# A ternary feed-forward kernel: gelu in PSUM in the last block, its last chunk in halves, one more block of x kept on chip, the first result in two pieces

## The chip, the core and the metric

The kernel runs on one core of one Trainium2 chip. The metric is the time of one execution on the device, in microseconds; the figure of a kernel is the median of several executions. The profile is of one further execution, and its span (first to last instruction) is a little shorter than that execution's time. Engines: TensorE (PE, matmuls), VectorE (DVE), ScalarE (ACT), GpSimd (POOL) and SyncE (SP); DMA engines move data between the device memory and the on-chip memory SBUF. PSUM is the on-chip memory that matmuls write.

## What is computed

x has 128 items of 64 channels by 512 features. Each item picks one of 200 condition matrices (64 x 64) by its index and is multiplied by it. The result goes through two ternary linear layers (512 to 2048 to 512) with an exact gelu between them; the output is rounded to 4 bits with one scale for the whole tensor and added to x:

```python
w = weights[conditions]
c = jnp.einsum('bct,bcd->bdt', x, w)
h = ternary_linear(c, W1, b1)            # W -> alpha * sign(W) * (|W| > delta)
h = jax.nn.gelu(h, approximate=False)
y = ternary_linear(h, W2, b2)
scale = jnp.max(jnp.abs(y)) / QMAX + EPS
q = jnp.clip(jnp.round(y / scale), -QMAX, QMAX) * scale
out = x + q
```

The scale is a maximum over all of y, so no output can be written before the last y is known. x is needed twice: at the start of a block, and again at the end for the sum.

## The kernel before

**Tiling.** The 128 items are 16 blocks (NB) of 4 pairs (PAIRS), so a block is 512 tokens (BLK), and its x is 128 partitions x 4 x 512 fp32, 1 MiB. The 2048 hidden units are 16 chunks (NH) of 128. Every fp32 operand of a matmul is split in two parts, high (a rounded copy made by ACT) and low (the remainder, made by DVE), so that each product takes two matmuls.

**A step.** Blocks 0, 1, 13, 14 and 15 run in plain steps, eight(s), one for each block n and chunk hc. A step widens the fp8 weights of the next chunks (widen1, widen2, on POOL), runs layer1 (8 matmuls of 128x512 into a PSUM tile ph), then bend: ACT applies gelu to ph and writes the result to an SBUF buffer hf, ACT copies that to the high part, DVE subtracts for the low part. At the end of the step layer2 runs 8 matmuls for the chunk of two steps ago (LAG = 2) into the four PSUM tiles py of the block. Blocks 2 to 12 (SEVEN) use a scheme with seven products in place of eight; the change doesn't touch them.

**After a block's last chunk** result moves each py to an SBUF tile y with alpha and bias (four DVE operations), and largest takes the maxima. For block 14 this happens in step 1 of block 15. The y of all 15 earlier blocks stay on chip in the pool big; block 15's y stays in PSUM.

**Loads of x for the end.** In block 15, room comes free and x is loaded again: block 0 into a big tile (hc == 0), blocks 1 and 2 into tiles of the pool half (hc == 1, 2), blocks 3 and 4 in quarters into the dead fp8 weights (lend, lines 817 to 821). After the last step blocks 5 and 6 go into the two big tiles of block 15's conditioned input, blocks 7, 8 and 9 into half tiles (split_x, line 999), and blocks 10 to 15 into tiles that come free as results leave. All these DMAs are issued by SP, in the order written, so a load that waits for room holds those behind it.

**The end.** The last three chunks of layer 2 are done pair by pair (lines 977 to 984), the maxima are spread over the partitions by a transpose (spread) and give scale and its inverse; then for each half block ACT computes q = y * inverse into int8, DVE computes q * scale + x into y, and POOL issues the DMA to the output. POOL has at most eight output DMAs on their way.

**Pools.** half has 10 tiles of 128 x 1024 fp32. In block 15 they hold the widened weights of layer 1 and layer 2, hf (two buffers in one tile, line 669), the parts of h, and x. PSUM has eight banks of 128 x 512 fp32: two for ps_c (conditioning), two for ps_h (ph), four for ps_y (py).

**Order.** Instructions of an engine stay in the order in which the program writes them (InOrder); an engine that waits holds everything behind it. All operations are issued through one helper, which is why the profile shows line 55 for nearly everything; tiles are told apart by name.

Of the kernel before, what the change touches and what calls it, by code (L numbers as in the profile page):

```python
# [29 lines left out]
F32 = mybir.dt.float32  # L30
# [5 lines left out]
AF = mybir.ActivationFunctionType  # L36
ALU = mybir.AluOpType
# [3 lines left out]
P = 128  # L41
# [17 lines left out]
def tile_cond_ternary_ffn(  # L59
# [12 lines left out]
    pe, act, dve, pool, sp = (  # L72
        InOrder(tc, e) for e in (nc.tensor, nc.scalar, nc.vector, nc.gpsimd, nc.sync)
    )
    B, C, T = x.shape
    S, _, D = weights.shape
    NT = T // P
    NH = W1.shape[1]
    assert 2 * C == P and 2 * D == P and C == D and W1.shape == (P, NH, NT, P)
    PAIRS = 4  # L80
    BLK = PAIRS * P
    NB = B // (2 * PAIRS)
# [5 lines left out]
    HALF = BLK // 2  # L88
# [5 lines left out]
    ps_c = ctx.enter_context(tc.tile_pool(name="ps_c", bufs=2, space=PSUM))  # L94
    ps_h = ctx.enter_context(tc.tile_pool(name="ps_h", bufs=2, space=PSUM))
# [3 lines left out]
    out_blk = out.rearrange("(n j p) c t -> n (p c) j t", j=PAIRS, p=2)  # L99

    def pair_of_pairs(h):
        return slice(h * PAIRS // 2, (h + 1) * PAIRS // 2)

    def load_x(n):

        xt = big.tile([P, PAIRS, T], F32, tag="big", name=f"xt_{n}")
        for h in range(2):
            js = pair_of_pairs(h)
            sp.dma_start(out=xt[:, js, :], in_=x_blk[n][:, js, :])
        return [xt[:, pair_of_pairs(h), :] for h in range(2)]  # L110

    def half_x(n, h):

        xt = half.tile([P, PAIRS // 2, T], F32, tag="half", name=f"xt_{n}_{h}")
        sp.dma_start(out=xt, in_=x_blk[n][:, pair_of_pairs(h), :])
        return xt

    def split_x(n):

        return [half_x(n, h) for h in range(2)]  # L120
# [14 lines left out]
    for g in range(NG):  # L135
        w = big.tile([P, GH, T], F32, tag="big", name=f"nat1_{g}")
# [6 lines left out]
    for g in range(NG):  # L143
        w = big.tile([P, GH, T], F32, tag="big", name=f"nat2_{g}")
# [36 lines left out]
    diag = const.tile([P, PAIRS, P], F32)  # L181
# [44 lines left out]
        split(pc, *(t[:, :, j * P : (j + 1) * P] for t in two))  # L226


    def spread(top1, out, wide_top):

        dve.tensor_copy(wide_top, top1.to_broadcast([P, P]))
        tops = ps_c.tile([P, P], F32, tag="pc", name=f"tops_{out.name}")
        pe.transpose(tops, wide_top, ident_f)
        return tops

# [21 lines left out]
    def flat(w):  # L257
        return w.rearrange("p a b -> p (a b)")
# [107 lines left out]
    cond = {0: two_next}  # L366


    hidden = {}
    wide1 = {}  # L370
# [30 lines left out]
            pool.tensor_copy(w, w2t[:, hc])  # L401
        wide2[n, hc] = w

    def layer1(n, hc, ph, pieces=1, between=None):

        w = wide1.pop((n, hc))
        for i in range(pieces):
            part = slice(i * BLK // pieces, (i + 1) * BLK // pieces)
            for c in range(NT):
                if between is not None and c == NT - 1:  # L410
                    between()
                for k in range(2):
                    pe.matmul(
                        out=ph[:, part],
                        lhsT=w[:, c, :],
                        rhs=cond[n][k][:, c, part],
                        start=(c == 0 and k == 0),
                        stop=(c == NT - 1 and k == 1),
                    )

    def bend(n, hc, ph, two, hf, engine=dve):
        act.activation(hf, ph, AF.Gelu, bias=b1t[:, hc : hc + 1], scale=alpha[1])
        if engine is None:
            act.copy(two[0], hf)
            open_low[n, hc] = lambda: dve.tensor_tensor(two[1], hf, two[0], ALU.subtract)
        else:
            split(hf, *two, engine)
        hidden[n, hc] = two
# [42 lines left out]
    def early(hc, between=None):  # L471

        slot = (hc + 1) % 5
        if slot < 2:
            ph = ps_h.tile([P, BLK], F32, tag="ph", name=f"ph_0_{hc}")
        else:
            ph = ps_y.tile([P, BLK], F32, tag=f"py{slot - 2}", name=f"ph_0_{hc}")
        layer1(0, hc, ph, 2 if hc == 0 else 1, between)
        waiting[hc] = ph

    def early_bend(hc):
# [187 lines left out]
    hf = ring[:2]  # L669
# [142 lines left out]

    steps = [(n, hc) for n in range(NB) for hc in range(NH)]
    again = []
    dying = [flat(t).bitcast(F32).rearrange("p (j t) -> p j t", j=PAIRS) for t in (w1t, w2t)]

    def lend(t, n, hc):
# [5 lines left out]
    def eight(s):  # L823

        n, hc = steps[s]
        if s + 1 < len(steps):
            ahead = steps[s + 1]
            if ahead[0] not in SEVEN:
                widen1(*ahead)
                lend(0, *ahead)  # L830
            else:
                for g in (2, 3, 0):
                    widen7(0, g)
        widen2(*steps[s + 1 - LAG])
        lend(1, *steps[s + 1 - LAG])
        if n + 1 < NB:
            if hc == 0:
                if n + 1 == SEVEN[0]:
                    extra["x"] = half.tile([P, 2, T], F32, tag="half", name="x_quarters")
                    for j in range(2):  # L840
                        quarter_x(n + 1, j)
                else:
                    x_next.append(load_x(n + 1) if n + 1 < NB - 1 else split_x(n + 1))
                two_next.append(parts7(n + 1) if n + 1 in SEVEN else parts(n + 1))
            if 2 <= hc < 2 + PAIRS:
                fetched.append(fetch(n + 1, hc - 2))
            if 7 <= hc < 7 + PAIRS:
                place(hc - 7, fetched[hc - 7 - PAIRS])
        if n == NB - 1 and hc == 0:
            again.append(load_x(0))  # L850
        if n == NB - 1 and hc in (1, 2):
            again.append(split_x(hc))
        ph = ps_h.tile([P, BLK], F32, tag="ph", name=f"ph_{n}_{hc}")
        layer1(n, hc, ph)
        two = half.tile([P, 2, BLK], F32R, tag="half", name=f"h_{n}_{hc}")
        bend(n, hc, ph, [two[:, k, :] for k in range(2)], hf[hc % 2])
        if s + 1 < len(steps) and steps[s + 1][0] in SEVEN and n not in SEVEN:
            widen7(0, 1)
        if n + 1 < NB and 8 <= hc < 8 + PAIRS:
            j = hc - 8  # L860
            if n + 1 in SEVEN:
                condition7(n + 1, j, extra["x"][:, j % 2, :], two_next[-1])()
                if j + 2 < PAIRS:
                    quarter_x(n + 1, j + 2)
            else:
                condition(n + 1, j, pair_of(x_next[-1], j), two_next[-1])
            cond[n + 1] = two_next[-1]
        if hc == LAG:
            for j in range(PAIRS):
                largest(n - 1, j)  # L870
        if n + 1 == SEVEN[0]:
            if hc == 2:
                extra["making"] = combine()
            if hc in (3, 4, 5, 6):
                next(extra["making"])
        if s == len(steps) - 1:
            return
        if s == NH + 1:
            alpha_2()
        layer2(*steps[s - LAG])  # L880
        if steps[s - LAG][1] == NH - 1:
            for j in range(PAIRS):
                result(n - 1, j)
# [64 lines left out]
    s = NH  # L948
    finish = None
    parting = []  # L950
    while s < len(steps):
        n, hc = steps[s]
# [14 lines left out]
    n = NB - 1  # L967
# [9 lines left out]
    for j in range(PAIRS):  # L977
        for hc in range(NH - 1 - LAG, NH):
            layer2(n, hc, [j])
        y = ypsum[n][j]  # L980
# [6 lines left out]
    ymax1 = const.tile([P, 1], F32)  # L987
# [1 line left out]
        ymax1, ymax.rearrange("p n j -> p (n j)")[:, n * PAIRS : NB * PAIRS + 1], AX.X, ALU.max  # L989
    )  # L990
    scale = const.tile([P, 1], F32, name="scale")
    tops = spread(ymax1, scale, diag[:, 0, :])
    dve.tensor_reduce(scale, tops, AX.X, ALU.max)
    dve.tensor_scalar(scale, scale, 1.0 / QMAX, EPS, ALU.mult, ALU.add)
    inverse = const.tile([P, 1], F32)
    dve.reciprocal(inverse, scale)


    xs = again + [split_x(len(again) + i) for i in range(3)]
    quant = flat(diag).bitcast(I8).rearrange("p (k t) -> p k t", k=PAIRS)  # L1000
    AHEAD = len(xs)
    for n in range(NB):

        while len(xs) < min(AHEAD + 3 * n // 2, NB):
            xs.append(load_x(len(xs)))
        for h in range(2):


            q = quant[:, h * PAIRS // 2 : (h + 1) * PAIRS // 2, :]
            if n < NB - 1:  # L1010
                y = res = ys[n][:, pair_of_pairs(h), :]
                act.activation(flat(q), flat(y), AF.Identity, scale=inverse)
                dve.scalar_tensor_tensor(
                    flat(y), flat(q), scale, flat(xs[n][h]), ALU.mult, ALU.add
                )
            else:
                res = xs[n][h]
                for k in range(PAIRS // 2):
                    y = ypsum[n][h * PAIRS // 2 + k]
                    act.activation(q[:, k, :], y, AF.Identity, scale=inverse)  # L1020
                    dve.scalar_tensor_tensor(
                        res[:, k, :], q[:, k, :], scale, res[:, k, :], ALU.mult, ALU.add
                    )
            pool.dma_start(out=out_blk[n][:, pair_of_pairs(h), :], in_=res)
# [44 lines left out]
```

## Time and profile before

| | |
|---|---|
| median of 3 runs | 1062.01 us (1061.17 to 1062.29) |
| profiled execution, its time | 1061.88 us |
| its span | 1059.5 us |
| mean granted TensorE clock | 0.969 |
| busy: PE | 986.9 us (93%) |
| busy: PEld (weight load) | 864.2 us (82%) |
| busy: DVE, ACT, POOL | 609.5, 611.3, 627.2 us |
| bytes moved | 62.19 MB, of which 44.34 MB read and 16.78 MB written in device memory |
| DMA of x (xt<-in_x, 512 KB each) | 36 issues, median 6.9 us to landing |
| DMA of results (out<-y, 512 KB each) | 30 issues, median 12.5 us to landing |

Busy time is the sum of an engine's instructions over the span. The page also cuts the span into 40 equal slices, each of 26.5 us, and gives each engine's busy share there in tenths; a row PEclk gives the granted clock, a row DMA the mean busy share of the 16 DMA engines. In a list of groups or a timeline, "out<-in" names the tile written and the tiles read, "128x512" is partitions by elements, and the bracket at the end is how long the engine sat idle before the instruction and who released it. The operations that the change touches, by kind and size, with their mean length:

| engine, operation | size | count | mean ns |
|---|---|---|---|
| ACT gelu, ring<-ph | 128x512 | 80 | 779 |
| ACT cast, h<-ring (SBUF to SBUF) | 128x512 | 256 | 621 |
| ACT cast, x<-pc (PSUM to SBUF) | 128x512 | 20 | 583 |
| ACT copy, ring<-z (PSUM to SBUF) | 128x512 | 88 | 588 |
| ACT copy, ring<-xy (PSUM to SBUF) | 128x256 | 176 | 370 |
| DVE subtract, h<-ring,h | 128x512 | 252 | 771 |
| DVE subtract, x<-pc,x | 128x512 | 20 | 684 |
| DVE subtract, xb<-pc,xb | 128x256 | 44 | 413 |
| ACT q, diag<-y | 128x1024 | 30 | 1148 |
| ACT q, diag<-py | 128x512 | 4 | 684 |
| DVE sum, y<-diag,scale,xt | 128x1024 | 26 | 1282 |
| DVE sum, xt<-diag,scale,xt | 128x512 | 4 | 748 |

### The profile page before, as it was taken

The page shows a single profiled execution, that of the slowest core. Times are in us where ns is not written, and L with a number is a line of the kernel's source. Part 1 is how long each engine was busy: PE and PEld are TensorE (multiplying, and loading weights), DVE is VectorE, ACT ScalarE, POOL GpSimd, SP SyncE. Part 2 cuts the span into 40 slices and gives each one's busy share as a digit, 9 for nine tenths or more (in the row PEclk, how much of TensorE's full clock was granted, in tenths as well). Part 3 has the DMA queues.
Part 4 walks back from the last instruction along what each step waited for, and adds up shares of the span by engine and source line. Part 5 has one row for each costly group of instructions (what it writes and reads, how often), then busy time and mean ns, then how long its engine had stood idle before and what let it go on. Part 6 is the DMA issues. An engine that isn't in the chain of part 4 may idle for free.

```text
span 1059.5 us, 16719 instructions
## 1 busy us (share of the span) xinstructions
PE 986.9 (93%) x5760; PEld 864.2 (82%) x5761; DVE 609.5 (58%) x1078; ACT 611.3 (58%) x1040; POOL 627.2 (59%) x1016
## 2 busy tenths in 40 slices
PE   8999999999999999999999999999999999999400
PEld 5877889999999999999999999999998888888300
DVE  7896646565656565565656565666645224232682
ACT  7993546666656666666666666666654433343481
POOL 6865656675766666676766666676764435333242
PEclk9999999999999999999999999999999999999755
DMA  9100100001000000100000000101001010041899
GB/s 363 56 21 4 32 13 14 32 5 31 15 22 24 17 28 15 31 6 32 15 22 23 14 32 12 33 6 30 16 22 43 3 40 6 1 149 37 297 413 373
DMA packets 26611, 62.19 MB, mean 59 GB/s; under 512 B 3488, under 2 KB 3488, under 8 KB 25760
## 3 DMA queue, kind: packets, MB, share of 16 engines
q1 hardware_dynamic: 19872, 42.25, 11.7%
q0 software_dynamic: 6656, 18.88, 4.6%
q8 instruction: 46, 0.75, 0.3%
q14 instruction: 37, 0.30, 0.1%
HBM read 44.34 MB, written 16.78 MB: 58 GB/s over the span
## 4 chain that ended last, share of the span: by engine, by line
PE 90%; DVE 4%; DMA 3%; ACT 1%; issue 1%; SPq 1%; POOL 0%; POOLq 0%; DVEq 0%; ACTq 0%
PE py L55 42%; PE xy L55 16%; PE ph L55 13%; PE z L55 12%; PE pc L55 5%; DMA xt<-in_x 3%; PE idle L55 1%; DVE h L55 1%; DVE y L55 1%; ACT diag L55 1%; DVE junk L55 1%; SPq L55 1%; DVE terns L55 0%; PE number L55 0%; DVE ymax L55 0%
## 5 line engine op out<-in xcount | busy, mean ns | idle before, releaser
L55 PE MATMUL py<-wf,h 128*128 128x512 f32 x2048 | 531.2, 395 | 0.9 <-ACT h L55 0.7
L55 PEld LDWEIGHTS py<-wf,h 128*128 128x128 f32 x2048 | 365.3, 189 | 65.2 <-DVE y L55 2.0
L55 DVE TENSOR_TENSOR h<-ring,h 128x512 fp32r<-128x512 f32 x252 | 193.5, 771 | 185.0 <-ACT h L55 185.0
L55 POOL CAST wf<-w2t 128x512 fp32r<-128x512 fp8e4 x242 | 172.1, 711 | 153.7 <-PE py L55 150.0
L55 ACT ACTIVATE ring<-ring,b1t,alpha_w 128x512 f32<-128x512 f32 x176 | 144.3, 820 | 97.9 <-DVE ring L55 97.9
L55 POOL CAST wf<-w1s 128x256 fp32r<-128x256 fp8e4 (+1 forms) x264 | 132.1, 505 | 110.6 <-PE xy L55 80.5
L55 POOL CAST wf<-w1t 128x256 fp32r<-128x256 fp8e4 (+1 forms) x240 | 158.7, 666 | 58.1 <-PE ph L55 46.5
L55 ACT CAST h<-ring 128x512 fp32r<-128x512 f32 x256 | 158.9, 621 | 8.3
L55 PE MATMUL ph<-x,wf 128*128 128x512 f32 (+1 forms) x648 | 157.5, 388 | 0.3 <-DVE x L55 0.3
L55 ACT ACTIVATE ring<-ph,b1t,alpha_w 128x512 f32<-128x512 f32 x80 | 62.3, 779 | 141.7 <-PE ph L55 141.6
L55 PEld LDWEIGHTS ph<-x,wf 128*128 128x128 f32 x648 | 120.1, 188 | 25.7 <-POOL wf L55 0.6
L55 DVE TENSOR_TENSOR ring<-xy,ring 128x256 f32<-128x256 f32 (+1 forms) x176 | 97.2, 552 | 64.3 <-PE xy L55 64.3
L55 PEld LDWEIGHTS xy<-xt,wf 128*128 128x128 f32 x704 | 107.6, 189 | 14.1
L55 PE MATMUL xy<-xb,wf 128*128 128x256 f32 x704 | 112.4, 281 | 0.0
L55 PE MATMUL xy<-xt,wf 128*128 128x256 f32 x704 | 111.8, 282 | 0.0
L55 PEld LDWEIGHTS xy<-xb,wf 128*128 128x128 f32 x704 | 102.2, 190 | 7.9
L55 ACT COPY ring<-xy 128x256 f32<-128x256 f32 x176 | 65.1, 370 | 68.4 <-PE xy L55 68.4
L55 PE MATMUL z<-xt,wf 128*128 128x256 f32 x704 | 98.3, 282 | 0.0
L55 ACT COPY ring<-z 128x512 f32<-128x512 f32 x88 | 51.7, 588 | 73.2 <-DVE h L55 71.1
L55 PEld LDWEIGHTS z<-xt,wf 128*128 128x128 f32 x704 | 90.2, 190 | 0.0
L55 DVE TENSOR_TENSOR xt<-x_quarters,xt 128x512 fp32r<-128x512 f32 x44 | 33.8, 768 | 91.2 <-ACT xt L55 91.2
L55 POOL DMA_INDIRECT wg<-in_L_cond_weights,rows x64 | 73.3, 1146 | 11.7 <-issue 4.9
(103 smaller groups left out, 852.8 us busy)
## 6 DMA issues: line engine op xcount, KB each, us to landing
xt<-in_x SPq DMA_DIRECT2D x36, 512.0 KB, 6.9
out<-y POOLq DMA_DIRECT2D x30, 512.0 KB, 12.5
x_quarters<-in_x SPq DMA_DIRECT2D x48, 256.0 KB, 2.6
nat<-in_L_ffn_W SPq DMA_DIRECT2D x6, 1024.0 KB, 10.2
nat<-in_L_ffn_W SPq DMA_DIRECT2D x3, 512.0 KB, 8.8
wg<-in_L_cond_weights,rows POOLq DMA_INDIRECT x64, 2.6
w1t<-in_x SPq DMA_DIRECT2D x4, 256.0 KB, 2.5
w2t<-in_x SPq DMA_DIRECT2D x4, 256.0 KB, 2.6
```

Source lines behind the costliest of these rows:

```text
L55: return lambda *args, **kw: self._tc.keep_in_program_order(make(*args, **kw))
```

## The change

In block 15 gelu writes its result back into ph, in PSUM, and the cast and the subtraction read it there; the SBUF tile of hf is then free after block 14. The last chunk of block 15 runs layer 1 for tokens 0 to 255 and then for tokens 256 to 511, each half in a ph tile of its own with its own gelu, cast and subtraction. In step 1 of block 15 SP loads half 0 of block 7's x into a half tile and ACT copies it into the two banks of ps_c; in step 3 half 1 is loaded into a half tile. The transpose of the maxima takes its bank from ps_h instead of ps_c. After the last step blocks 5, 6, 8, 9 and 10 are loaded, and 11 to 15 later. The first half block of the output is computed and written in two pieces of 128x512. layer1 takes the part of the tokens as an argument in place of a number of pieces; the order of block 0's first chunk is the same as before.

```diff
--- before.py
+++ after.py
@@ -226,10 +226,10 @@
         split(pc, *(t[:, :, j * P : (j + 1) * P] for t in two))
 
 
-    def spread(top1, out, wide_top):
+    def spread(top1, out, wide_top, pool=ps_c, tag="pc"):
 
         dve.tensor_copy(wide_top, top1.to_broadcast([P, P]))
-        tops = ps_c.tile([P, P], F32, tag="pc", name=f"tops_{out.name}")
+        tops = pool.tile([P, P], F32, tag=tag, name=f"tops_{out.name}")
         pe.transpose(tops, wide_top, ident_f)
         return tops
 
@@ -401,22 +401,21 @@
             pool.tensor_copy(w, w2t[:, hc])
         wide2[n, hc] = w
 
-    def layer1(n, hc, ph, pieces=1, between=None):
-
-        w = wide1.pop((n, hc))
-        for i in range(pieces):
-            part = slice(i * BLK // pieces, (i + 1) * BLK // pieces)
-            for c in range(NT):
-                if between is not None and c == NT - 1:
-                    between()
-                for k in range(2):
-                    pe.matmul(
-                        out=ph[:, part],
-                        lhsT=w[:, c, :],
-                        rhs=cond[n][k][:, c, part],
-                        start=(c == 0 and k == 0),
-                        stop=(c == NT - 1 and k == 1),
-                    )
+    halves = slice(0, HALF), slice(HALF, BLK)
+
+    def layer1(n, hc, ph, part=slice(0, BLK), between=None):
+        w = wide1[n, hc]
+        for c in range(NT):
+            if between is not None and c == NT - 1:
+                between()
+            for k in range(2):
+                pe.matmul(
+                    out=ph,
+                    lhsT=w[:, c, :],
+                    rhs=cond[n][k][:, c, part],
+                    start=(c == 0 and k == 0),
+                    stop=(c == NT - 1 and k == 1),
+                )
 
     def bend(n, hc, ph, two, hf, engine=dve):
         act.activation(hf, ph, AF.Gelu, bias=b1t[:, hc : hc + 1], scale=alpha[1])
@@ -475,7 +474,8 @@
             ph = ps_h.tile([P, BLK], F32, tag="ph", name=f"ph_0_{hc}")
         else:
             ph = ps_y.tile([P, BLK], F32, tag=f"py{slot - 2}", name=f"ph_0_{hc}")
-        layer1(0, hc, ph, 2 if hc == 0 else 1, between)
+        for part in halves if hc == 0 else [slice(0, BLK)]:
+            layer1(0, hc, ph[:, part], part, between)
         waiting[hc] = ph
 
     def early_bend(hc):
@@ -812,6 +812,8 @@
 
     steps = [(n, hc) for n in range(NB) for hc in range(NH)]
     again = []
+
+    IN_PSUM, kept_x = 7, []
     dying = [flat(t).bitcast(F32).rearrange("p (j t) -> p j t", j=PAIRS) for t in (w1t, w2t)]
 
     def lend(t, n, hc):
@@ -848,12 +850,25 @@
                 place(hc - 7, fetched[hc - 7 - PAIRS])
         if n == NB - 1 and hc == 0:
             again.append(load_x(0))
+        if n == NB - 1 and hc == 1:
+            stage = half_x(IN_PSUM, 0)
+            for k in range(PAIRS // 2):
+                kept_x.append(ps_c.tile([P, T], F32, tag="pc", name=f"x_psum_{k}"))
+                act.copy(kept_x[k], stage[:, k, :])
         if n == NB - 1 and hc in (1, 2):
             again.append(split_x(hc))
-        ph = ps_h.tile([P, BLK], F32, tag="ph", name=f"ph_{n}_{hc}")
-        layer1(n, hc, ph)
+        if n == NB - 1 and hc == 3:
+            kept_x.append(half_x(IN_PSUM, 1))
         two = half.tile([P, 2, BLK], F32R, tag="half", name=f"h_{n}_{hc}")
-        bend(n, hc, ph, [two[:, k, :] for k in range(2)], hf[hc % 2])
+        two = [two[:, k, :] for k in range(2)]
+
+        for part in halves if s == len(steps) - 1 else [slice(0, BLK)]:
+            ph = ps_h.tile([P, BLK], F32, tag="ph", name=f"ph_{n}_{hc}_{part.start}")
+            ph = ph[:, part]
+            layer1(n, hc, ph, part)
+
+            bend(n, hc, ph, [t[:, part] for t in two], ph if n == NB - 1 else hf[hc % 2])
+        hidden[n, hc] = two
         if s + 1 < len(steps) and steps[s + 1][0] in SEVEN and n not in SEVEN:
             widen7(0, 1)
         if n + 1 < NB and 8 <= hc < 8 + PAIRS:
@@ -989,14 +1004,16 @@
         ymax1, ymax.rearrange("p n j -> p (n j)")[:, n * PAIRS : NB * PAIRS + 1], AX.X, ALU.max
     )
     scale = const.tile([P, 1], F32, name="scale")
-    tops = spread(ymax1, scale, diag[:, 0, :])
+    tops = spread(ymax1, scale, diag[:, 0, :], ps_h, "ph")
     dve.tensor_reduce(scale, tops, AX.X, ALU.max)
     dve.tensor_scalar(scale, scale, 1.0 / QMAX, EPS, ALU.mult, ALU.add)
     inverse = const.tile([P, 1], F32)
     dve.reciprocal(inverse, scale)
 
 
-    xs = again + [split_x(len(again) + i) for i in range(3)]
+    xs = again + [[None, kept_x.pop()]]
+    xs += [split_x(len(xs) + i) for i in range(2)] + [[half_x(len(xs) + 2, 0)]]
+    xs[-1].append(half_x(len(xs) - 1, 1))
     quant = flat(diag).bitcast(I8).rearrange("p (k t) -> p k t", k=PAIRS)
     AHEAD = len(xs)
     for n in range(NB):
@@ -1009,10 +1026,25 @@
             q = quant[:, h * PAIRS // 2 : (h + 1) * PAIRS // 2, :]
             if n < NB - 1:
                 y = res = ys[n][:, pair_of_pairs(h), :]
+                if n == 0 and h == 0:
+
+                    for k in range(PAIRS // 2):
+                        act.activation(q[:, k, :], y[:, k, :], AF.Identity, scale=inverse)
+                        dve.scalar_tensor_tensor(
+                            y[:, k, :], q[:, k, :], scale, xs[n][h][:, k, :], ALU.mult, ALU.add
+                        )
+                        pool.dma_start(out=out_blk[n][:, k, :], in_=y[:, k, :])
+                    continue
                 act.activation(flat(q), flat(y), AF.Identity, scale=inverse)
-                dve.scalar_tensor_tensor(
-                    flat(y), flat(q), scale, flat(xs[n][h]), ALU.mult, ALU.add
-                )
+                if xs[n][h] is None:
+                    for k in range(PAIRS // 2):
+                        dve.scalar_tensor_tensor(
+                            y[:, k, :], q[:, k, :], scale, kept_x[k], ALU.mult, ALU.add
+                        )
+                else:
+                    dve.scalar_tensor_tensor(
+                        flat(y), flat(q), scale, flat(xs[n][h]), ALU.mult, ALU.add
+                    )
             else:
                 res = xs[n][h]
                 for k in range(PAIRS // 2):
```

## Prediction

> **What bounds the kernel now.** The page's 40 slices come first: they tell where one limit ends and the next begins.
>
> ```profile
> span 1059.5 us, 16719 instructions
> PE   8999999999999999999999999999999999999400
> DMA  9100100001000000100000000101001010041899
> ```
>
> TensorE is at 9 for 37 slices; then it stops, and the DMA row, near 0 until then, goes to 8 and 9 for the last three. The kernel is two stages: matmuls up to about 987 us, then a tail that adds x and writes the output. I cut the tail into stretches (columns: stretch, length, busy us and count of PE, PEld, DVE, ACT, POOL, granted clock, DMA share, GB/s):
>
> ```profile
> 988.00:989.00 1.00, 1.00 (x6) 0.81 (x5) 0.96 (x2) 0.00 (x0) 0.00 (x0) 1.00 0.79 240
> 990.00:991.00 1.00, 1.00 (x6) 0.84 (x5) 0.98 (x2) 0.00 (x0) 0.00 (x0) 1.00 0.90 301
> 998.00:999.00 1.00, 0.00 (x0) 0.00 (x0) 1.00 (x1) 1.00 (x1) 0.77 (x1) 0.50 1.05 385
> 1020.00:1030.00 10.00, 0.00 (x0) 0.00 (x0) 9.06 (x8) 9.18 (x9) 3.87 (x6) 0.50 1.04 416
> 1056.00:1057.00 1.00, 0.00 (x0) 0.00 (x0) 0.00 (x0) 0.00 (x0) 0.00 (x0) 0.50 0.69 279
> ```
>
> From about 986 until 1056.7 the DMA engines are full, but for some 0.3 us of holes at 988 to 991. While only x is read they move about 387 GB/s (998), once outputs are written too about 415 (1020). The chain of waits agrees: its largest piece in the tail is a DMA of x. Bytes set the end, not the arithmetic. Next the timeline where the stages meet and where the last block begins (start, length, engine, work, [idle before <- what ended it]):
>
> ```profile
> 926.61 1.91 SPq L55 DMA_DIRECT2D xt<-in_x  x4
> 934.10 0.78 ACT L55 ACTIVATE ring<-ph,b1t,alpha_w 128x512 f32<-128x512 f32 x1 [2.19 <-PE ph L55]
> 935.56 0.69 DVE L55 TENSOR_TENSOR h<-ring,h 128x512 fp32r<-128x512 f32 x1 [2.94 <-ACT h L55]
> 936.17 2.72 DVE L55 SCALAR_TENSOR_TENSOR y<-py,alpha_w,b2b 128x512 f32<-128x512 f32 x4
> 938.95 0.30 PEld L55 LDWEIGHTS py<-wf,h 128*128 128x128 f32 x2 [0.33 <-DVE y L55]
> ...
> 985.08 0.78 ACT L55 ACTIVATE ring<-ph,b1t,alpha_w 128x512 f32<-128x512 f32 x1 [2.19 <-PE ph L55]
> 985.10 44.11 SPq L55 DMA_DIRECT2D xt<-in_x  x22
> 986.65 0.47 PE L55 MATMUL py<-wf,h 128*128 128x512 f32 x1 [0.70 <-ACT h L55]
> ...
> 998.21 0.77 POOL L55 DMA_DIRECT2D out<-y  x1 [13.56 <-DVE y L55]
> ```
>
> Three things: the tail's 22 loads start at 985.10, when the last layer-1 matmul frees the block's input; the first output leaves 13 us later; and at 938.95 PE waits for DVE's y, so there a delay on ACT or DVE has no cover.
>
> **What the Trainium skill says.** "DMA: Bandwidth & Descriptors", section "Issuing engines are not separate DMA queues": queues started by different engines run on the same 16 DMA engines and interleave. The trace agrees: with loads (SP) and outputs (POOL) together the share stays at 1.02 to 1.06 and the rate at about 415 GB/s, so a byte less in either is time off the end. "ScalarE: Activation LUTs", section "Step-by-step: what each stage is for": ACT reaches PSUM faster than SBUF. No row of before writes PSUM from ACT; reads agree (cast from PSUM 583 ns against 621 from SBUF, 128x512). "VectorE: DVE Perf Modes", section "The perf-mode tier table (the rule you actually need)": an fp32 tensor_tensor runs in the 1x mode whether an operand is in PSUM or not. The trace agrees: 684 ns for x<-pc, 690 for h<-ring undisturbed.
>
> **The change part by part.**
>
> *One more block of x on chip.* The tail before loads blocks 5 to 15 (11 blocks) and writes 16, each block 128x4x512 fp32 = 1.0486 MB. After, block 7 is loaded in the last block: half 0 through an SBUF stage into two PSUM banks, half 1 into the buffer that the gelu gave up. The tail moves 26 blocks instead of 27: 1.0486 MB / 0.415 = 2.53 us less. This is the sum's main term. The added load falls at 927 to 940, where the DMA engines idle between bursts: nothing.
>
> *Gelu in PSUM.* On 16 chunks gelu, cast and subtraction work on ph instead of SBUF: gelu about 0.74 to 0.78 (not shown before; 0.78 is the SBUF row), cast 0.58 for 0.62, subtraction 0.69. A ph bank is now held until the subtraction ends, not only until gelu: chunk finished 955.99, subtraction over 958.22, the bank wanted again at 961.3: 3.1 us to spare. The second half of the last chunk needs the bank of chunk 14 at about 984.2; chunk 14's subtraction ends at 983.61: 0.6 to spare. Cost nothing.
>
> *The copies to PSUM, an added wait.* ACT's two copies stand between the cast of chunk 0 and the gelu of chunk 1 and wait for the stage's load. That load is third behind block 0's two halves in SP's queue, and landings show first in, first out, 1.3 us apart. For the issues of 927.6 and 928.1 the trace has:
>
> ```profile
> L55 SPq DMA_DIRECT2D xt<-in_x x2: 419/420/420, 927.6 to 928.1; - x2
> DMA to landing us min/median/max: 5.4/5.8/6.2
> ```
>
> Third landing: 927.6 + 5.4 = 933.0. Two copies at about 0.6 (the 621 ns row; 0.55 to 0.65) end at 934.2 to 934.3; gelu of chunk 1 began at 934.10. So it is late by 0.15, of which faster casts return 0.05. Queued behind it: the subtraction of 935.56, behind that DVE's four y of block 14, and PE waits for the last of them already. 0.1 us passes on to PE; between 0 and 1.0 if the landing is up to 0.9 later.
>
> *Last chunk in halves.* 16 matmuls 128x256 instead of 8 of 128x512. Groups of four in the middle blocks start 0.47 to 0.48 apart (600.40 to 600.87), so 0.119 each: 16 x 0.119 = 1.90 against 1.81, +0.09 on the release of the loads. In return half a's gelu (0.78 - 0.22 = 0.56 by the 588 and 370 ns of 512 and 256 wide copies), cast 0.38 and subtraction 0.41 are over at 985.6, half b's at 986.6, while PE's matmuls of chunks 13 and 14 cover 985.13 to 986.03. The wait of 0.70 and the 0.16 after it vanish; the first py is done so that DVE starts at 986.83, not 987.84: 1.0 us. DVE's 8 operations of py (5.6 us) and the scale then end 1.0 earlier, at 994.3. But that is worth nothing by itself as long as loads fill the DMA engines: what is late next is the loads.
>
> *First result in pieces.* ACT 0.71 + DVE 0.75 instead of 1.15 + 1.28: 1.0 us earlier again. First output issue 998.21 - 1.0 - 1.0 = about 996. Needed: the tail now has only 4.5 blocks that can load at once (5, 6, 8, 9, half of 10; the rest wait for DVE to finish a block 1 half, about 999.6): 4.72 MB / 0.39 from 986.1, done at about 998.2 to 999. Outputs are on the queue from 997; no hole. Its gain: 2.2 us of read-only traffic at 387 run at 415 instead, 2.2 x 28/415 = 0.15 us. One more POOL issue (0.73) and two DVE operations from PSUM for block 7 (2 x 0.75 for 1.28) lie in stretches where POOL and DVE wait for DMA: nothing. *tops* moved to ps_h finds a free bank: nothing.
>
> **Sum**, on the profiled execution (1061.88, span 1059.5; the median 1062.01 is 0.13 above): -2.53 - 0.15 + 0.09 + 0.10 = -2.5 us. DMA ends at 1054.2 instead of 1056.7, and the span 2.8 later as before, at 1057.0. Median 1062.0 - 2.5 = 1059.5.
>
> **Rivals.**
> A. As summed: -2.5, own range 1058.9 to 1060.0. For it: the DMA share over 1.0 to the end.
> B. The saving is partly eaten at the seam. Block 8's first load waits for PE's last py group (about 989.7) where block 7's was free at 987.2, and the read-ahead is half a block shorter: a hole of 0.5 to 1.5 us. For it: 240 GB/s at 988 with loads queued. Against: each tail load lands 5 to 9 us after its issue, so some are always queued. -2.5 + 1.3: 1060.8.
> C. More than bytes. The holes of 988 to 991 close and reads, done earlier, leave a longer write-only end (420 GB/s at 1052 to 1056): up to -1.0 more: 1058.5.
> D. Slower. One mechanism: ACT's copies wait for the stage's landing, and the whole chain gelu, subtraction, four y, PE moves with it one for one. It pays off the 2.5 us only if the landing is later than 935.5, and is slower by over 0.2% from about 937.6, 10 us after its issue. For it: nothing covers the wait. Against: 5.4 measured in that place with the same queue ahead. With 939: about 1065.
>
> **How the numbers follow.** A 0.62, B 0.22, C 0.12, D 0.04. Predicted: A, 1059.5. The range: from C's 1058.5 to a little past B, 1060.9. 0.2% is 2.1 us (about what a measurement can tell), so faster means under 1059.9: nine tenths of A (0.55), C (0.12) and a little of B (0.03): 0.70. Same: 0.26. Slower 0.04.
>
> **What would show it.** Right: no hole in the DMA share from 986 on, one load of x less there (10 blocks), first output at about 996, DMA ending near 1054.2, PE's wait of 0.70 gone, ACT's copies at 933.0 to 934.3. Wrong: a share under 0.9 between 990 and 1001 (B); a PE gap near 938 over 0.5 us (D); rates over 420 GB/s (C).

## The result, and the profile after

Run beside each other, 8 executions each, the kernel before takes 1061.51 us (median) and the changed kernel 1059.11 us. The ratio is 0.9975, with a 95% interval from 0.9966 to 0.9983: 2.4 us less, where 2.5 were forecast. The profiled execution is the shortest of the eight, 1058.49 us, and its span is 1056.6.

The page of the changed kernel, in the lines that were shown of before:

```profile
span 1056.6 us, 16741 instructions
PE   8999999999999999999999999999999999999500
DMA  9100100100000010101000010101001010051799
```

The shape is the same: matmuls, then three slices of DMA. What changed lies in the tail. The stretches of the changed kernel (columns: stretch, length, busy us and count of PE, PEld, DVE, ACT, POOL, granted clock, DMA share, GB/s):

```profile
988.00:989.00 1.00, 1.00 (x6) 0.84 (x5) 0.96 (x3) 0.00 (x0) 0.00 (x0) 1.00 1.03 356
...
998.00:999.00 1.00, 0.00 (x0) 0.00 (x0) 1.00 (x1) 0.99 (x1) 0.72 (x1) 0.50 1.06 391
1001.00:1002.00 1.00, 0.00 (x0) 0.00 (x0) 0.98 (x2) 0.95 (x2) 0.51 (x2) 0.50 0.98 303
1002.00:1004.00 2.00, 0.00 (x0) 0.00 (x0) 2.00 (x2) 1.84 (x2) 1.23 (x2) 0.50 1.02 377
...
1020.00:1030.00 10.00, 0.00 (x0) 0.00 (x0) 9.92 (x9) 9.18 (x9) 3.56 (x5) 0.50 1.03 415
...
1053.00:1054.00 1.00, 0.00 (x0) 0.00 (x0) 0.00 (x0) 0.00 (x0) 0.00 (x0) 0.50 0.92 369
1054.00:1055.00 1.00, 0.00 (x0) 0.00 (x0) 0.00 (x0) 0.00 (x0) 0.00 (x0) 0.50 0.39 160
```

The plateau is at 415 GB/s as before, and DMA ends at about 1054.4 instead of 1056.7. From 1001 to 1004 the rate sinks to 303 and 377 GB/s, while the share stays near 1: the share doesn't show such a dip, the bytes do. The kernel before has dips too, 240 and 301 GB/s at 988 and 990 and 350 GB/s at 1002, and so has a second profile of the changed kernel (below), with 191 and 330 GB/s at 988 and 989 and 408 at 1001. The timeline of the changed kernel, at the start of the last block and where the stages meet:

```profile
926.62 2.44 SPq L55 DMA_DIRECT2D xt<-in_x  x5
932.96 1.11 ACT L55 COPY x_psum<-xt 128x512 f32<-128x512 f32 x2 [1.11 <-DMA xt<-in_x]
934.11 0.75 ACT L55 ACTIVATE ph<-ph,b1t,alpha_w 128x512 f32<-128x512 f32 x1
935.52 0.69 DVE L55 TENSOR_TENSOR h<-ph,h 128x512 fp32r<-128x512 f32 x1 [2.93 <-ACT h L55]
936.12 2.72 DVE L55 SCALAR_TENSOR_TENSOR y<-py,alpha_w,b2b 128x512 f32<-128x512 f32 x4
937.54 2.10 PE L55 MATMUL py<-wf,h 128*128 128x512 f32 x8
938.89 0.30 PEld L55 LDWEIGHTS py<-wf,h 128*128 128x128 f32 x2 [0.25 <-DVE y L55]
939.48 2.01 PE L55 MATMUL ph<-x,wf 128*128 128x512 f32 x8
...
984.95 5.63 PE L55 MATMUL py<-wf,h 128*128 128x512 f32 x24
985.02 16.07 SPq L55 DMA_DIRECT2D xt<-in_x  x12
995.93 1.22 POOL L55 DMA_DIRECT2D out<-y  x2 [11.42 <-DVE y L55]
```

ACT's copies run from 932.96 to 934.07, and gelu of chunk 1 starts at 934.11, where it started at 934.10 before: the new wait fits with nothing to spare. The last 24 matmuls run without a stop; the waits of 0.70 and 0.16 are gone. The first output leaves at 995.93 instead of 998.21.

### The profile page after: what moved, and what is told of

Same layout as the page of the kernel before. It is cut to its first block, busy times and chain, and to the rows that moved or that the text cites. A ratio compares the mean times of both kernels' runs of the same rounds, so it can differ in the third digit from the quotient of the medians.

```text
span 1056.6 us, 16741 instructions
## 1 busy us (share of the span) xinstructions
PE 985.9 (93%) x5768; PEld 864.5 (82%) x5769; DVE 609.9 (58%) x1081; ACT 612.0 (58%) x1045; POOL 625.6 (59%) x1017
## 4 chain that ended last, share of the span: by engine, by line
PE 89%; DVE 5%; DMA 3%; ACT 1%; issue 1%; SPq 0%; POOLq 0%; DVEq 0%; ACTq 0%
PE py L55 42%; PE xy L55 16%; PE ph L55 13%; PE z L55 12%; PE pc L55 5%; DMA out<-y 3%; DVE y L55 1%; DVE h L55 1%; ACT diag L55 1%; DMA nat<-in_L_ffn_W 1%; DVE top L55 1%; DVE junk L55 1%; DVE terns L55 0%; PE number L55 0%; DVE ymax L55 0%
## 5 line engine op out<-in xcount | busy, mean ns | idle before, releaser
L55 DVE TENSOR_TENSOR h<-ring,h 128x512 fp32r<-128x512 f32 x236 | 182.7, 777 | 142.7 <-ACT h L55 142.7
L55 POOL CAST wf<-w2t 128x512 fp32r<-128x512 fp8e4 x242 | 169.6, 701 | 152.0 <-PE py L55 148.1
L55 ACT CAST h<-ring 128x512 fp32r<-128x512 f32 x240 | 148.9, 621 | 7.8
L55 ACT ACTIVATE ring<-ph,b1t,alpha_w 128x512 f32<-128x512 f32 x64 | 49.8, 778 | 106.3 <-PE ph L55 106.2
L55 ACT COPY ring<-z 128x512 f32<-128x512 f32 x88 | 51.7, 588 | 73.6 <-DVE h L55 71.4
```

What stands on the lines that cost most here:

```text
L55: return lambda *args, **kw: self._tc.keep_in_program_order(make(*args, **kw))
```

## The experiments

All were timed beside the kernel before, on one chip but for the last. Each has one profile, of one of its executions. Two theories stood against each other at first. A: the bytes in the tail decide, and what happens where the stages meet is covered by queued loads. S: the seam (the microseconds in which the matmuls end and the tail's loads and first outputs begin) pays, that is, the earlier end of PE and the earlier first output shorten the end.

**Without block 7 on chip.** All other parts of the change stay:

```diff
-        if n == NB - 1 and hc == 1:
-            stage = half_x(IN_PSUM, 0)
...
-        if n == NB - 1 and hc == 3:
-            kept_x.append(half_x(IN_PSUM, 1))
...
-    xs = again + [[None, kept_x.pop()]]
...
+    xs = again + [split_x(len(again) + i) for i in range(3)]
```

> Block 7 is not kept on chip; gelu in PSUM, the halves, the result in pieces stay. Theory A (the tail is paid by its bytes): 27 blocks move in the tail again, so the 2.5 us are lost and only closed holes and a little earlier mixing remain: 0 to 0.5 us under before, about 1061.2, with DMA ending near 1056.5. Rival S (the seam pays: PE's end and the first output are 2.2 us earlier, and that shortens the end): 1.0 to 2.2 us under before, 1059.3 to 1060.5.

Measured: 1061.07 us, ratio to before 0.9994 (0.9985 to 1.0002), which is no clear gain over the kernel before. By medians it is 0.7 us (1061.74 to 1061.07), more than A's 0.5 and less than S's 1.0. Its last stretches:

```profile
1055.00:1056.00 1.00, 0.00 (x0) 0.00 (x0) 0.00 (x0) 0.00 (x0) 0.00 (x0) 0.50 1.01 414
1056.00:1057.00 1.00, 0.00 (x0) 0.00 (x0) 0.00 (x0) 0.00 (x0) 0.00 (x0) 0.50 0.32 127
```

DMA is full until 1056.3, though the first output leaves at 995.66, 2.5 us before that of the kernel before. With five blocks of loads ready, an earlier seam buys little: A, with its range missed by 0.2 us, comes nearer than S, and S falls as a theory of the whole gain.

**The changed kernel once more**, on the chip of the other experiments.

> The changed kernel once more, beside the others on one chip. Both theories: 0.9975 of the kernel before, about 1059.1.

Measured: 1059.31 us, 0.9976 (0.9968 to 0.9985). Against the experiment above block 7 is worth 1061.07 - 1059.31 = 1.8 us. In the profiles, from the first load of the tail to DMA's end, it is 984.9 to 1056.3 = 71.4 us there and 985.1 to 1054.2 = 69.1 us here: 2.3 us (2.0 with the first profile of the changed kernel, 985.0 to 1054.4).

**One more block less.** Block 14's x is not loaded:

```diff
-            xs.append(load_x(len(xs)))
+            xs.append(xs[13] if len(xs) == 14 else load_x(len(xs)))
```

> Block 14's x is not loaded for the sum; block 13's x is added there instead, so the tail moves 25 blocks. Theory A: another 1.0486 MB at 0.415 MB per us: 2.5 us under the changed kernel, about 1056.6. Rival S, or an end bound by DVE, POOL or the landing of the last load: less than 1 us gained, over 1058.

Measured: 1057.15 us, 0.9955 (0.9941 to 0.9968): 2.2 us under the changed kernel. A again; neither DVE nor POOL nor a landing bounds the end. It is a little less than 2.5. The profile here is of the longest of the five executions (1058.12 us); its last microseconds move 381, 242 and 156 GB/s from 1051 to 1054, but whether the shorter ones end like this isn't shown.

**The last chunk whole, block 7 on chip.**

```diff
-        for part in halves if s == len(steps) - 1 else [slice(0, BLK)]:
+        for part in [slice(0, BLK)]:
```

> The last chunk of layer 1 whole again, all else as in the changed kernel. Both: PE waits 0.7 to 0.9 us again, and the scale and the first output are about 1.1 us later (997.0). Theory A: the loads queued since 985 cover that, so within 0.3 us of the changed kernel, 1058.8 to 1059.4. Rival S: 1.0 us slower, about 1060.1.

Measured: 1060.02 us, 0.9984 (0.9978 to 0.9991); that is 0.7 us over the changed kernel's 1059.31. A expected at most 0.3, S 1.0. The profile of this kernel shows two dips:

```profile
993.00:994.00 1.00, 0.00 (x0) 0.00 (x0) 0.93 (x3) 0.00 (x0) 0.00 (x0) 1.00 0.84 229
...
1003.00:1004.00 1.00, 0.00 (x0) 0.00 (x0) 0.98 (x2) 0.95 (x2) 0.65 (x1) 0.50 0.77 229
```

Block 8's first load is issued at 991.5, not 989.7 to 989.8, since the tile it takes comes free with a late py matmul; and the first output leaves at 997.48. The next load that needs a result first, the second half of block 10, is issued at 1000.6, where the changed kernel issues it at 999.0; from 1002 to 1003 nearly all the bytes moved (0.29 of 0.32 MB) are of outputs. So A as first put is not the whole: with half a block less of loads ready, the seam is covered only just.

**The first result whole, halves kept.**

```diff
-                if n == 0 and h == 0:
+                if False:
```

> Only the first result is whole again; last chunk in halves, block 7 on chip. First output about 997. Theory A with a seam (bytes decide, but with only 4.5 blocks of loads ready a first output that comes 1 us later leaves the DMA engines short of work near 1001 to 1004): 0.4 to 0.9 us slower than the changed kernel, 1059.5 to 1060.0, with a GB/s dip there. Rival (the halves gain through PE alone and the seam is covered): 1059.1.

Measured: 1059.40 us, 0.9978 (0.9969 to 0.9986): no difference from 1059.31, though the first output leaves only at 997.13 and the profile has a shallow dip (334 to 354 GB/s from 1002 to 1006). By itself this part is worth nothing that can be measured; the seam reading that was added to A expected 0.4 at least, and missed. The profiles suggest why. An output that is issued while loads are queued waits for them: in the changed kernel the first one is issued at 995.93 and moves no byte before 998.8, here it is issued at 997.13 and moves none before 999.2, and up to there the loads keep the DMA engines full (a share of 1.05). And the second half of block 10 is issued at 999.4 here, nearly as early as in the changed kernel.

**Both whole.** The two edits above together.

> The last chunk and the first result whole again, block 7 still on chip. Both: first output at about 998.1. Theory A: the 4.5 blocks that can be loaded at once last until about 998.5, so a hole of 0 to 0.6 us in the DMA share near 999 and 1059.1 to 1059.8. Rival S: 2 us slower than the changed kernel, about 1061.1.

Measured: 1060.43 us, 0.9988 (0.9981 to 0.9994), 1.1 us over the changed kernel, with a deep dip:

```profile
1002.00:1003.00 1.00, 0.00 (x0) 0.00 (x0) 1.00 (x2) 0.84 (x2) 0.67 (x1) 0.50 1.03 246
1003.00:1004.00 1.00, 0.00 (x0) 0.00 (x0) 1.00 (x1) 1.00 (x1) 0.72 (x1) 0.50 0.92 260
```

Against 415 GB/s these two microseconds lack (169 + 155) / 415 = 0.8 us of work. The halves and the pieces together guard 1.1 us of what block 7 brings. Whether they would guard as much without block 7 can be read from four profiles, two lines each (985 to 1000 and 1000 to 1010): the kernel before, the one without block 7, the changed kernel (second profile), and this one.

```profile
985.00:1000.00 15.00, 6.47 (x26) 4.31 (x24) 10.69 (x18) 5.59 (x6) 1.37 (x2) 0.79 0.96 345
1000.00:1010.00 10.00, 0.00 (x0) 0.00 (x0) 9.91 (x9) 9.18 (x9) 5.82 (x9) 0.50 1.04 406
985.00:1000.00 15.00, 5.77 (x25) 4.28 (x24) 12.54 (x22) 6.62 (x9) 2.59 (x4) 0.79 0.97 346
1000.00:1010.00 10.00, 0.00 (x0) 0.00 (x0) 9.92 (x10) 9.18 (x8) 5.71 (x8) 0.50 1.03 414
985.00:1000.00 15.00, 5.98 (x27) 4.49 (x25) 12.33 (x21) 6.71 (x9) 2.60 (x4) 0.78 0.98 343
1000.00:1010.00 10.00, 0.00 (x0) 0.00 (x0) 9.92 (x9) 9.19 (x9) 5.72 (x8) 0.50 1.03 412
985.00:1000.00 15.00, 6.68 (x26) 4.44 (x25) 10.64 (x18) 5.49 (x6) 1.32 (x2) 0.81 0.96 329
1000.00:1010.00 10.00, 0.00 (x0) 0.00 (x0) 9.92 (x9) 9.18 (x9) 5.82 (x9) 0.50 1.02 364
```

Over the 25 us that is 369, 373, 371 and 343 GB/s. With five blocks of loads ready (the first two) the halves and pieces change little; with 4.5 ready (the last two) they hold 28 GB/s, or 25 x 28 / 415 = 1.7 us of work, of which 1.1 us shows in the medians. It is one execution of each.

**The stage's load last in the queue.** SP issues block 1's halves before the load on which ACT's copies wait:

```diff
         if n == NB - 1 and hc == 1:
+            again.append(split_x(hc))
             stage = half_x(IN_PSUM, 0)
...
-        if n == NB - 1 and hc in (1, 2):
+        if n == NB - 1 and hc == 2:
             again.append(split_x(hc))
```

> SP issues block 1's two halves before the load that ACT's copies wait for, so that it is fifth in the queue and lands at 935.6 instead of 932.9. Theory D (nothing covers this wait; gelu, subtraction, the four y and PE move with it one for one): ACT's second gelu starts at 936.7 instead of 934.1, PE stands about 2.6 us near 938 to 942, and the end comes 2.4 to 2.7 us later, about 1061.7. Rival (the two chunks of LAG cover it): under 0.5 us, 1059.6 at most.

Measured: 1062.85 us, 1.0006 (0.9998 to 1.0014) of before, 3.5 us over the changed kernel, where D expected 2.4 to 2.7. Five of the 13 executions took 1061.06 to 1061.95 us, the other eight 1062.73 to 1063.62, and the profile is of the longest. The whole last block stands 0.7 us later in it than in the first profile of the changed kernel; the timeline, ACT first, then PE:

```profile
936.73 1.11 ACT L55 COPY x_psum<-xt 128x512 f32<-128x512 f32 x2 [4.15 <-DMA xt<-in_x]
937.78 0.74 ACT L55 ACTIVATE ph<-ph,b1t,alpha_w 128x512 f32<-128x512 f32 x1
...
940.66 3.60 PE L55 MATMUL py<-wf,h 128*128 128x512 f32 x8 [2.24 <-DVE y L55]
944.10 2.00 PE L55 MATMUL ph<-x,wf 128*128 128x512 f32 x8
```

Less the 0.7, gelu is 2.9 us late and PE's layer 2 2.4 us (940.66 - 0.73 against 937.54), so the delay passes on nearly one for one, as rival D had it. Then the eight matmuls take 3.60 us instead of 2.10, and PE's next layer 1 is 3.9 us late (944.10 - 0.73 against 939.48). The granted clock (the column before the DMA share) tells where the 1.5 us come from:

```profile
940.00:941.00 1.00, 0.34 (x1) 0.37 (x2) 1.00 (x2) 0.40 (x1) 0.00 (x0) 0.77 1.02 295
941.00:942.00 1.00, 1.00 (x3) 0.79 (x3) 1.00 (x3) 0.00 (x0) 0.00 (x0) 0.50 1.01 393
942.00:943.00 1.00, 1.00 (x4) 0.72 (x3) 1.00 (x2) 0.00 (x0) 0.00 (x0) 0.50 0.30 102
943.00:944.00 1.00, 1.00 (x4) 0.81 (x3) 1.00 (x3) 0.00 (x0) 0.00 (x0) 0.52 0.00 0
944.00:945.00 1.00, 1.00 (x5) 0.81 (x5) 1.00 (x3) 0.00 (x0) 0.61 (x1) 1.00 0.00 0
```

After the gap TensorE is granted half its clock for some 3 us. The mean clock of the whole execution is 0.970 to 0.971 in the five shorter executions, whose middle one is 2.0 us over the changed kernel, and 0.969 in the eight longer ones; so the lost clock may belong to those alone, but only one was profiled. D's wait is real; the changed kernel escapes it because its load is third in the queue.

**Layer 1 of the last chunk earlier.** It runs whole, before layer 2 of chunk 12, and blocks 5 and 6 are loaded as soon as it ends:

```diff
+        if s == len(steps) - 2:
+            return
         if s == len(steps) - 1:
+            layer2(*steps[s - 1 - LAG])
             return
...
+    last = [load_x(5 + i) for i in range(2)]
     lend(1, n, NH - 1)
...
-    for _ in range(2):
-        again.append(load_x(len(again)))
```

(Also the weights of chunk 14 go to the free buffer of layer 1, and the last chunk isn't halved.)

> Layer 1 of the last chunk, whole, runs before layer 2 of chunk 12, so that blocks 5 and 6 can be loaded at 983.2 instead of 985.0; PE's own end stays within 0.3 us. If only the start of the full stretch and the bytes counted: 1.8 us faster, 1057.3. With the seam (the first output does not move, and the same 4.5 blocks of loads run out 1.8 us sooner): most is lost again in a dip near 999 to 1003, 0 to 0.7 us faster, 1058.4 to 1059.1.

Measured: 1059.17 us, 0.9977 (0.9967 to 0.9986): no gain. PE's end didn't stay in place, though the expectation said so: the cast of chunk 15 had to wait for its tile until chunk 12 was used up, and the first output leaves at 996.83. The loads start at 983.61, and two dips take it back:

```profile
991.00:992.00 1.00, 0.68 (x4) 0.22 (x2) 0.96 (x3) 0.00 (x0) 0.00 (x0) 1.00 0.79 193
992.00:993.00 1.00, 0.00 (x0) 0.00 (x0) 0.97 (x2) 0.00 (x0) 0.00 (x0) 1.00 0.78 96
...
1002.00:1003.00 1.00, 0.00 (x0) 0.00 (x0) 0.98 (x2) 0.95 (x2) 0.52 (x2) 0.50 1.03 203
```

**Block 11's load before block 10's second half**, alone, and together with the early layer 1:

```diff
-    xs[-1].append(half_x(len(xs) - 1, 1))
...
             xs.append(load_x(len(xs)))
+        if n == 1:
+            xs[10].append(half_x(10, 1))
```

> SP issues block 11's load before the second half of block 10's: block 11 waits only for the sum of block 0, done 1.2 us before the sum that frees a tile for block 10's half. Seam theory (what is ready to move when the first loads run out is worth time as far as the GB/s dip near 1001 to 1004 goes, which is 0 to 0.6 us in the changed kernel): 0 to 0.4 us faster, 1058.9 to 1059.3. Theory of bytes alone: 1059.3.

> The early layer 1 of the last chunk and block 11 before block 10's second half together. With the early layer 1 alone the loads began 1.5 us sooner and two dips (991 to 993 and 1001 to 1004, some 0.5 MB each) took it back. Seam theory: the second dip shrinks, 0.5 to 1.0 us faster than with the early layer 1 alone, 1058.2 to 1058.7. If the dips are not for want of work: no change, 1059.2.

Measured: alone 1059.01 us, 0.9975 (0.9966 to 0.9983), no difference that can be told from the changed kernel. Together 1058.57 us, 0.9968 (0.9957 to 0.9980): the best of all by median, 0.7 us under the changed kernel, though the intervals overlap. Of the two dips of the early layer 1 the first stays (nothing moves at all from 991 to 992: block 8's load, issued at 990.17 when its tile came free, moves its first bytes at 992.0), the second is shallower:

```profile
991.00:992.00 1.00, 0.04 (x1) 0.00 (x0) 0.97 (x3) 0.00 (x0) 0.00 (x0) 1.00 0.00 0
1000.00:1001.00 1.00, 0.00 (x0) 0.00 (x0) 1.00 (x2) 0.84 (x2) 0.42 (x2) 0.50 0.93 272
1001.00:1002.00 1.00, 0.00 (x0) 0.00 (x0) 0.98 (x2) 0.95 (x2) 0.57 (x1) 0.50 0.94 305
```

**The first dip filled as well.** Layer 2 of chunk 13 runs for all pairs before chunk 15, so that block 8 finds its tile at 987.76:

```diff
     for j in range(PAIRS):
-        for hc in range(NH - 1 - LAG, NH):
-            layer2(n, hc, [j])
+        if j == 0:
+            layer2(n, NH - 3, [0])
+            layer2(n, NH - 2, [0])
+            layer2(n, NH - 3, range(1, PAIRS))
+        else:
+            layer2(n, NH - 2, [j])
+        layer2(n, NH - 1, [j])
```

> As the one before (early layer 1, block 11 first), and layer 2 of chunk 13 runs for all four pairs while PE waits for chunk 15's h, so that its tile is free at about 987.8 and block 8's first load leaves then, not at 990.2. The 1.3 us in which the DMA engines stood still at 990.7 to 992 close; PE's first py ends up to 0.7 us later and the first output with it. Seam theory: 0.3 to 0.9 us faster than 1058.57, 1057.7 to 1058.3. If the later output costs as much as the closed hole gains: 1058.6.

Measured: 1059.66 us, 0.9976 (0.9966 to 0.9986), on another chip: the ratio to before is that of the changed kernel again, and neither outcome that was written down came true. The first dip did close; the loads then ran out before the first output, which left at 997.57:

```profile
991.00:992.00 1.00, 0.00 (x0) 0.00 (x0) 0.97 (x3) 0.00 (x0) 0.00 (x0) 1.00 1.03 352
...
998.00:999.00 1.00, 0.00 (x0) 0.00 (x0) 0.83 (x1) 1.00 (x2) 0.71 (x2) 0.50 0.40 156
999.00:1000.00 1.00, 0.00 (x0) 0.00 (x0) 1.00 (x2) 0.69 (x2) 0.26 (x1) 0.50 0.81 309
1000.00:1001.00 1.00, 0.00 (x0) 0.00 (x0) 0.98 (x2) 0.95 (x2) 0.52 (x2) 0.50 0.49 123
1001.00:1002.00 1.00, 0.00 (x0) 0.00 (x0) 1.00 (x2) 0.84 (x2) 0.67 (x1) 0.50 1.07 145
1002.00:1003.00 1.00, 0.00 (x0) 0.00 (x0) 1.00 (x1) 1.00 (x1) 0.71 (x1) 0.50 0.63 236
```

This is the clearest picture of the seam. The loads that need no result first are 4.5 blocks, 4.72 MB, 12.2 us at 387 GB/s. Begin them earlier without earlier results, and the same work is only done sooner and followed by a hole.

## Why the prediction was right, and where not

The time, its direction and the likeliest case A came out: -2.4 us against -2.5. By its steps:

- *Block 7, -2.53.* The mechanism is shown twice, by giving the block back and by taking one more away. The term was too large: 1.8 us by medians (2.0 to 2.3 by the full stretch of the profiles) for the first, 2.2 for the second. Some of what is missing lies in a drain at the end that is less sharp (369 and 160 GB/s in the last two microseconds, where before had 422 and 279). The seam doesn't account for it: from 985 to 1010 the kernel before moves 369 GB/s on average, and the changed kernel 369 and 371 in its two profiles.
- *The seam, "no hole" and "worth nothing by itself".* There are holes, but in sum no more than before. One profile of the changed kernel lacks (415 - 303)/415 + 2 x (415 - 377)/415 = 0.45 us of work from 1001 to 1004, the other (387 - 191)/387 + (387 - 330)/387 = 0.65 us at 988 and 989. The holes of before were read from the share as 0.3 us; by the rate those of 988 and 990 are (387 - 240)/387 + (387 - 301)/387 = 0.6 us. The step that failed is the price of nothing for the halves. Once block 7 is on chip, a whole chunk costs 0.7 us, and with the whole first result 1.1. The prediction looked at when the output comes and at block 8's tile, but not at how a later PE end moves the loads that need a result first: the second half of block 10 is issued at 999.0 in the changed kernel and at 999.4 with the first result whole, which cost nothing, but at 1000.6 and 1000.5 in the two kernels with the chunk whole.
- *Earlier mixing, -0.15.* Not told apart from the rest: without block 7 all other parts of the change together bring 0.7 us by medians (1061.74 to 1061.07), with an interval that holds no change. Its mechanism was wrong in one point: an earlier issue of the first output doesn't start the mixing while loads are queued. Without block 7 it is issued at 995.66, and no output moves a byte before 999.6. That the sum came out so close owes something to luck: the block brought less than priced, the rest more.
- *The added wait, +0.10.* ACT's copies took 0.56 us each, not 0.6, and landed where the trace of before put them (933.0), so that gelu came at 934.11: cost nothing. PE's wait behind it fell from 0.33 to 0.25. In the second profile the copies begin at 933.20 and gelu at 934.24, and PE's wait is 0.31.
- *The halved matmuls, +0.09.* The 16 matmuls take 1.93 us on the chain of waits, against 1.83 for the eight before: as priced. Gelu in PSUM took 0.75 us and the cast 0.59, and no ph bank was waited for.
- *Rival D* was priced at one for one. The experiment on the queue shows nearly that (2.9 us on ACT, 2.4 on PE), and 1.5 us more from the clock in the profiled execution.
- *What would show it:* a DMA share under 0.9 was named as the sign of a hole. It is a poor one; the share was 0.98 where the rate had fallen to 303 GB/s. (TensorE's row of before, by the way, is at 9 in 36 slices, not 37; nothing rests on it.)

What stays open: how the 0.7 us of the other parts without block 7 divides between gelu in PSUM, halves and pieces, or whether it is there at all; what else block 7's 1.8 us lack against 2.5; and whether the 0.7 us of the best version would stand with more executions.

## What to carry to other kernels

In this kernel's tail, which moves data almost without a pause, bytes and holes count: a first output 2.5 us earlier brought no clear gain while five blocks of loads were ready, and keeping the chunk and the first result whole, with the first output 2.3 us later, cost 1.1 us once only 4.5 were. So price such a change by its read-ahead, that is, the bytes that can be moved before the first result exists, over the rate, against the time until the loads that need a result can move. Count that time to the first bytes and not to the issue, which came some 2 to 3 us earlier here (990.17 and 992.0 for block 8 in one kernel; 999.0 and about 1002 for block 10 in the changed one). And look for holes in the GB/s, not in the share. When room for more data is found on chip, the read-ahead that remains gets shorter, and what was idle slack at the seam can start to decide, as it did here.

## What the runs showed of the hardware

- In the profiled execution with the stage's load last, a gap in TensorE's work cost more than its length: after 2.2 us without matmuls (938.4 to 940.66) the granted clock fell from 1.00 to 0.50 and stayed there until 944, and 8 matmuls took 3.60 us that take 1.98 where nothing holds them. In the kernel before, the stop of 0.70 us at the end of the last block left the clock at 1.00.
- A DMA share near 1 went with very different rates: 0.98 with 303 GB/s and 1.03 with 415 in the changed kernel, 1.07 with 145 in the last experiment.
- An output issued while loads were queued moved nothing until they were nearly done: 3.9 us after its issue without block 7 (995.66 to 999.6), 2.9 in the changed kernel (995.93 to 998.8), but 1.1 us in the last experiment, where the loads had nearly run out (997.57 to 998.7).
- Gelu of 128x512 took 0.75 us from PSUM to PSUM and 0.78 from PSUM to SBUF; the cast took 0.59 us from PSUM and 0.62 from SBUF.
